# Keys laid out in DRAM by GpSimd's own stores, means of the first dense stage as three products, and low parts of keys taken later

## The chip, the cores and the metric

The kernel runs on one core of one Trainium2 chip. Its time is device time in microseconds (us) of one execution. The kernel before takes 2951.6 us, the median of three runs (2944.76 to 2952.74).

## The reference, cut to what matters

The input `x` is four images of 384 channels by 48 x 48 places (2304 tokens an image), all float32. The layer is an attention whose queries get a local part from a convolution:

```
local  = depthwise_conv_7x7(x), scaled and shifted (batch norm)
x_norm = layernorm over channels of x
q, k, v = x_norm @ qkv_w.T + qkv_b          # 8 heads of 48
q      = q + layernorm over channels of local
out    = softmax(q @ k.T / sqrt(48)) @ v    # 2304 x 2304 per head
out    = x + (out @ proj_w.T + proj_b)
```

## The kernel before

Tokens are worked on in groups of 384 (8 image rows), six groups to an image, so 24 groups `t` in all. Heads are worked on in pairs, four pairs to an image; a pair's keys against a group's queries are twelve *slots*: four pairs, three slots each, six key blocks of 128 tokens to a slot.

**Dense stage.** Ahead of the attention of an image, `from_x` (L565) is run for its six groups. TensorE makes for a group the values (3 products), the keys (3, `u` = 0 to 2) and the queries (3); in later images also the output projection of the image before (3). Products are made two at a time: `both` (L634) takes the generator through its two halves, the TensorE half and the evacuation half. The dense stage of the first image (0 to 164 us) also makes the layer norm of the next group inside each group. The norm's mean over channels was a sum of three 128-channel chunks by two VectorE additions (L404, L405) and one product with a constant matrix (`mean`, L416), once for the values and once for their squares. In later images (`kv` stages) the norm goes another way, by `out` (L460, L461: a small store to DRAM and its read back, `parts` and `four`) and `few_in` (L470), which VectorE waits for in its order.

**High and low parts of keys.** Keys are kept as a rounded part and a remainder. ScalarE writes the rounded part `k[:, 0]` (L593). VectorE writes the remainder `k[:, 1]` (L596) in `low`, which reads the PSUM tile again. `low` is put in a list; `both` runs all that are in the list between its two halves, so one `both` after its product. Then `low` calls `keys_out`, which issues the stores. The tiles `k` are taken from the same five buffers (tag `pt`) as the exponentials `pt` of the attention.

**Layout of keys.** The score products (L881) want a *stack* `ks` of a pair: 128 rows of two halves of 2304, in which each head has its 48 rounded rows, its 48 remainder rows and, for the third product, remainder rows twice. Head pairs 0, 1, 2 come mostly whole out of `u` = 0, 1, 2; heads 6 and 7 (pair 3) come in 16-row pieces of all three. `keys_out` on SyncE's queue (SP) writes pair 0 straight into its stack in SBUF (8 DMAs a group, `stack_head`, L544 to L547) and all other parts to a DRAM tensor `keys` in head order (10 DMAs a group, L531, L532). So SP issues 18 DMAs for a group's keys. In the first attention group of each image GpSimd's queue builds the stacks of pairs 1 to 3 out of `keys` by `stack_head` (8 DMAs a pair, each over all 2304 tokens), and after that stores each of the four stacks to DRAM as `wide` (`keep_stack`, L551, 2304 KB each). From then on, a stack is read from `wide` in three thirds of 768 KB (`load_keys`, L558), in every group, one pair ahead. There are two stack buffers in SBUF.

**Attention.** In a slot, TensorE makes 36 score products (L881), ScalarE exponentiates (L889) and TensorE weighs the values (L896, 24). VectorE meanwhile does the 7 x 7 convolution of the next group, 147 operations `acc` (L288) a group, spread over the slots and the dense stage by `plan` (L358), which is given an estimate of VectorE's free time per point (`spare`, `spare_at_keys`). VectorE also makes the low part of the queries (L758), after which SP copies pieces of `qs` (L763, L765). The order on TensorE, VectorE and ScalarE is the order of the text; the orders on SP and GpSimd are made by the framework's scheduler. Every engine works its own instructions in order.

Of the kernel before, what the change touches and what calls it, by code (L numbers as in the profile page):

```python
# [16 lines left out]
P = 128  # L17
NH = 8
# [27 lines left out]
def unshifted_pass(  # L46
# [333 lines left out]
    class Norm:  # L380
# [33 lines left out]
        def mean(self, m=None):  # L414
            self.m = two_banks()[:, 0, :G] if m is None else m
            nc.tensor.matmul(self.m, lhsT=mean_w, rhs=self.buf[:, 0, :], start=True, stop=True)  # L416

# [99 lines left out]
    keys, values = {}, {}  # L517
    lows = []
# [19 lines left out]
    def place_keys(b, p):  # L538
        stacks[b, p] = big.tile([P, 2, N], HALF, tag="ks", name=f"ks{b}_{p}", bufs=2)

    def stack_head(b, p, j, head, at, queue):

        dst, r = stacks[b, p].bitcast(F32), 64 * j
        queue.dma_start(out=dst[r : r + HD, 0, at], in_=head[:, 0])  # L544
        queue.dma_start(out=dst[r + HD : r + 64, 0, at], in_=head[0:16, 1])
        for i in range(2):
            queue.dma_start(out=dst[r + 32 * i : r + 32 * i + 32, 1, at], in_=head[16:HD, 1])  # L547

    def keep_stack(b, p):
        wide[b, p] = dram.tile([P, 2, N], F32, tag=f"wide{p}", name=f"wide{b}_{p}")  # L550
        nc.gpsimd.dma_start(out=wide[b, p], in_=stacks[b, p].bitcast(F32))  # L551
# [12 lines left out]

    def from_x(b, g, before=None, ao=None):  # L565
# [6 lines left out]
        if g == 0:  # L572
            keys[b] = dram.tile([NH, HD, 2, N], F32, tag="keys", name=f"keys{b}")
# [399 lines left out]
    norm.sum()  # L973
    norm.mean(bank)
# [9 lines left out]
    norm.sum_squares()  # L984
    norm.mean()
    norm.root()
    both(making)
    convolve_first(4)
    norm.scale(norm.newton())
    both(making)  # L990
    convolve_first(7)
    for g in range(1, NG):

        last = g == NG - 1
        making = from_x(0, g)
        both(making)
        assert not last or n_first >= each - PE_TAPS
        norm = Norm(accs[0] if last else xn[0, g + 1])
        norm.sum()
# [10 lines left out]
        norm.sum_squares()  # L1010
        norm.mean()
# [12 lines left out]
    query_end(0)  # L1024
    high_queries(0, 0)
    low_queries(0, 0)
    gather_tails(*reversed(queries[0]))
# [3 lines left out]
    for t in range(NT):  # L1031
        b, g = divmod(t, NG)
        if g == 0 and b:
# [4 lines left out]
            for gk in range(NG):  # L1038
# [48 lines left out]
        for s in range(NSLOT):  # L1087
# [638 lines left out]
```

## Time and profile before

| what | value |
|---|---|
| median of three runs | 2951.6 us |
| the profiled execution's own time / its span | 2951.98 / 2950.2 us |
| TensorE (PE) busy / VectorE (DVE) busy | 2783.3 us (94%) / 2474.2 us (84%) |
| ScalarE (ACT) / GpSimd (POOL) busy | 1641.8 us (56%) / 244.9 us (8%) |
| mean granted TensorE clock | 0.97 |
| DMA | 431.71 MB in 191693 packets |
| first dense stage / kv stages | 0 to 164 / about 820 to 957, 1521 to 1657, 2219 to 2360 us |

The profile is of one execution. "Busy" counts an engine's instructions; SP and POOL also issue DMAs. A row of a timeline gives start and length in us, engine, line, operation, what is written and read, and in brackets the idle time of the engine before it and what ended it. A fp32 product is two recorded matmuls, so a mean's single product is "x2" and one over three chunks is "x6". A row of a table of stretches gives a stretch's length, then each engine's busy time in it (with the number of instructions), the granted clock, the DMA engines' busy share and GB/s.

### The profile page before, as it was taken

The numbers are of one execution on the slowest core, as the hardware profiler recorded it, in microseconds if no ns is written. First come the engines' busy times: TensorE is split into PE (matmuls) and PEld (weight loads), VectorE is DVE, ScalarE is ACT, GpSimd is POOL, SyncE is SP. The second block draws the span as 40 slices with busy tenths as digits, with TensorE's granted clock in tenths as the row PEclk, the third lists the DMA queues.
The fourth block names the chain that finished last, engine by engine and source line by source line (L and its number), as shares of the span: only waits on it lengthen the run. The fifth ranks groups of instructions, "written<-read, shape, count | busy, mean of one in ns | idle before, by whom it ended". The sixth has DMA issues, their size and how long they took to land.

```text
span 2950.2 us, 52742 instructions
## 1 busy us (share of the span) xinstructions
PE 2783.3 (94%) x19190; PEld 1749.7 (59%) x19190; DVE 2474.2 (84%) x4899; ACT 1641.8 (56%) x2638; POOL 244.9 (8%) x429
## 2 busy tenths in 40 slices
PE   8868899898899899999999979999999999999999
PEld 5445555565555556666665646666665555666665
DVE  7869998898899699998999969999988978898512
ACT  4235556566532466676652446667773255666662
POOL 1011000000000100100100101001000010100100
PEclk9989999999999999999999989999999999999999
DMA  6265444443535954455445764545453675544551
GB/s 134 58 159 168 143 127 138 118 141 120 147 87 139 228 167 143 143 175 153 144 109 146 175 190 147 170 145 152 154 149 92 168 187 180 159 141 155 167 172 62
DMA packets 191693, 431.71 MB, mean 146 GB/s; under 512 B 62592, under 2 KB 139328, under 8 KB 186304
## 3 DMA queue, kind: packets, MB, share of 16 engines
q0 software_dynamic: 42016, 254.84, 26.9%
q1 hardware_dynamic: 146416, 169.80, 23.6%
q8 instruction: 154, 2.52, 0.4%
q10 hardware_dynamic: 2992, 3.62, 0.3%
q14 instruction: 115, 0.94, 0.1%
HBM read 298.44 MB, written 86.02 MB: 130 GB/s over the span
## 4 chain that ended last, share of the span: by engine, by line
PE 67%; DVE 21%; DMA 10%; SPq 1%; issue 1%; ACT 1%; ACTq 0%; DVEq 0%
PE o L896 27%; PE r L881 23%; PE r L507 16%; DVE acc L288 14%; DMA parts<-part 4%; DMA four<-parts 2%; DMA qs<-qs 1%; DMA keys<-k 1%; DMA xn<-in_x_dram 1%; DVE ao L800 1%; DMA ks<-k 1%; DVE sq L405 0%; DVE qs L758 0%; DVE sq L456 0%; DVE sq L404 0%
## 5 line engine op out<-in xcount | busy, mean ns | idle before, releaser
L288 DVE SCALAR_TENSOR_TENSOR acc<-slab,vec,acc 128x368 f32<-128x368 f32 (+6 forms) x3447 | 1770.0, 584 | 1.2
L889 ACT ACTIVATE pt<-r 128x768 f32<-128x768 f32 x1728 | 1253.9, 827 | 208.9 <-PE r L881 148.5
L896 PE MATMUL o<-pt,v 128*64 128x384 f32 x6912 | 1184.9, 492 | 1.6 <-ACT pt L889 1.5
L881 PE MATMUL r<-qs,ks 64*128 64x384 f32 x10368 | 1037.1, 349 | 137.1 <-DMA qs<-qs 67.8
L881 PEld LDWEIGHTS r<-qs,ks 64*128 64x128 f32 x10368 | 922.5, 191 | 330.0 <-issue 252.0
L896 PEld LDWEIGHTS o<-pt,v 128*64 128x64 f32 x6912 | 472.1, 137 | 596.5 <-issue 511.4
L558 POOL DMA_DIRECT2D ks<-wide x240 | 173.6, 725 | 1723.4 <-PE r L881 1658.4
L781 ACT COPY o<-o 113x384 f32<-113x384 f32 x192 | 92.2, 480 | 378.5 <-PE o L896 378.4
L507 PE MATMUL r<-xn,w_qk 128*128 128x384 f32 x864 | 283.7, 486 | 0.0
L507 PEld LDWEIGHTS r<-xn,w_qk 128*128 128x128 f32 x864 | 164.2, 190 | 114.5
L507 PE MATMUL r<-w_v,xn 128*128 128x384 f32 x432 | 153.5, 509 | 15.7 <-DVE xn L502 15.2
L470 DVE TENSOR_REDUCE few<-four 128x12 f32<-128x48 f32 x80 | 18.6, 232 | 167.8 <-DMA four<-parts 167.6
L585 ACT COPY v<-r 128x384 f32<-128x384 f32 x72 | 32.1, 481 | 216.9 <-PE r L507 216.9
L507 PEld LDWEIGHTS r<-w_v,xn 128*128 128x128 f32 x432 | 84.8, 199 | 80.0 <-DVE xn L502 18.3
L800 DVE TENSOR_TENSOR ao<-ao,o 113x384 f32<-113x384 f32 x144 | 79.7, 553 | 57.7 <-ACT o L781 57.4
L507 PE MATMUL r<-af,w_o 128*128 128x384 f32 x360 | 119.1, 487 | 0.0
L791 ACT COPY ao<-o 113x384 f32<-113x384 f32 x72 | 34.4, 478 | 122.8 <-PE o L896 122.8
L758 DVE TENSOR_TENSOR qs<-xn,qs 128x384 fp32r<-128x384 f32 x72 | 39.9, 555 | 70.4 <-ACT qs L753 70.4
L507 PEld LDWEIGHTS r<-af,w_o 128*128 128x128 f32 x360 | 68.2, 190 | 47.8 <-issue 0.6
L610 ACT ACTIVATE xn<-r,qkb 128x384 f32<-128x384 f32 x72 | 41.5, 580 | 90.7 <-PE r L507 89.0
L593 ACT ACTIVATE k<-r,qkb 128x384 fp32r<-128x384 f32 x72 | 39.4, 580 | 63.4 <-PE r L507 51.8
L862 DVE SCALAR_TENSOR_TENSOR xr<-r,pb,xr 128x384 f32<-128x384 f32 x72 | 42.1, 612 | 35.8 <-PE r L507 20.0
(124 smaller groups left out, 963.4 us busy)
## 6 DMA issues: line engine op xcount, KB each, us to landing
ks<-wide POOLq DMA_DIRECT2D x240, 768.0 KB, 7.0
wide<-ks POOLq DMA_DIRECT2D x16, 2304.0 KB, 12.1
qs<-qs SPq DMA_DIRECT2D x528, 48.0 KB
keys<-k SPq DMA_DIRECT2D x96, 144.0 KB
ks<-keys POOLq DMA_DIRECT2D x48, 288.0 KB, 12.2
xr<-in_x_dram SPq DMA_DIRECT2D x24, 576.0 KB
slab<-in_x_dram SPq DMA_DIRECT2D x32, 378.0 KB
held<-ao SPq DMA_DIRECT2D x20, 576.0 KB
```

Of the source, the lines that this page charges most:

```text
L288: nc.vector.scalar_tensor_tensor(dst, src, weight, dst, ALU.mult, ALU.add)
L507: nc.tensor.matmul(dst, lhsT=weights(c), rhs=src(c), start=c == 0, stop=c == CC - 1)
L558: nc.gpsimd.dma_start(out=stacks[b, p].bitcast(F32)[:, :, at], in_=wide[b, p][:, :, at])
L593: nc.scalar.activation(k[:, 0, :], r[:, :G], AF.Identity, bias=bias)
L610: nc.scalar.activation(src[:, i, :], q[:, :G], AF.Identity, bias=qkb[:, 0, i : i + 1])
L758: nc.vector.tensor_sub(qs[:, 1, :], query_of(t, p), qs[:, 0, :])
L781: nc.scalar.copy(part[0 : 64 + HA], sums[0 : 64 + HA, 0, :G])
L800: nc.vector.tensor_add(dst, dst, part[0 : 64 + HA])
L862: nc.vector.scalar_tensor_tensor(xr[:, co, :], m, pb[:, co : co + 1], xr[:, co, :], ALU.add, ALU.add)
L881: nc.tensor.matmul(r[:, j, :G], lhsT=ks[rows, w, kb * P : (kb + 1) * P], rhs=qs[rows, m, :], start=i == 0, stop=i == 2,)
L889: nc.scalar.activation(pt, r[:, :, :G], AF.Exp, scale=SCALE)
L896: nc.tensor.matmul(sums[halves[j], 0, :G], lhsT=values[t // NG, kb // NB][:, first : first + 64], rhs=pt[:, j, :], start=i == 0, stop=i == ...
```

## The change

1. Keys of `u` = 1, 2 and all pieces of pair 3 are stored by GpSimd's queue from SBUF straight into the stack layout in DRAM (`wide[b, 1..3]`), 32 DMAs a group. SP keeps the 8 of pair 0. The tensor `keys` is gone.
2. `load_keys` always reads `wide` by thirds, in the first group of an image too. Only pair 0's stack is still stored from SBUF (`keep_stack(b)`, once an image, after slot 1).
3. In the first dense stage both means of a norm are a product over three chunks (`mean_by_chunk`), without VectorE's additions.
4. `both` no longer runs the low parts; `lows_out(n)` stands further back: in a `kv` group the first after convolve point 2 and the other two after point 3; in the first dense stage after `root` and after ten convolution operations; of that stage's last group, two after `low_queries(0, 0)`. `spare_at_keys` is changed to match, with the same sum.

```
     def spare_at_keys(b, g, h):
-        time = 4.6 - {0: 0.6, 1: 0.7, 2: 1.4, 4: 1.2}.get(h, 0.0)
+        time = 4.6 - {0: 0.6, 2: 0.7, 3: 1.4, 4: 1.2}.get(h, 0.0)
...
+        def mean_by_chunk(self, src, m=None):
+            self.m = two_banks()[:, 0, :G] if m is None else m
+            project(self.m, lambda c: mean_w, lambda c: src[:, c, :])
...
+    def stack_head(dst, j, k, queue):
+
+        r = 64 * j
+        queue.dma_start(out=dst[r : r + HD, 0], in_=k[r : r + HD, 0])
+        queue.dma_start(out=dst[r + HD : r + 64, 0], in_=k[r : r + 16, 1])
+        for i in range(2):
+            queue.dma_start(out=dst[r + 32 * i : r + 32 * i + 32, 1], in_=k[r + 16 : r + HD, 1])
 
     def keys_out(b, g, u, k):
         at = slice(g * G, (g + 1) * G)
         k = k.bitcast(F32)
-        if u == 0:
-            if g == 0:
-                place_keys(b, 0)
-            for j in range(2):
-                stack_head(b, 0, j, k[64 * j : 64 * j + HD], at, nc.sync)
+        if g == u == 0:
+            place_keys(b, 0)
+            for p in range(1, NP):
+                wide[b, p] = dram.tile([P, 2, N], F32, tag=f"wide{p}", name=f"wide{b}_{p}")
         for j in range(2):
-            r = 64 * j
-            if u:
-                nc.sync.dma_start(out=keys[b][2 * u + j, :, :, at], in_=k[r : r + HD])
-            nc.sync.dma_start(
-                out=keys[b][6 + j, 16 * u : 16 * u + 16, :, at], in_=k[r + HD : r + 64]
-            )
...
+            if u == 0:
+                stack_head(stacks[b, 0].bitcast(F32)[:, :, at], j, k, nc.sync)
+            else:
+                stack_head(wide[b, u][:, :, at], j, k, nc.gpsimd)
+        for j in range(2):
+            last, r = wide[b, NP - 1][64 * j : 64 * j + 64, :, at], 64 * j + HD
+            nc.gpsimd.dma_start(out=last[16 * u : 16 * u + 16, 0], in_=k[r : r + 16, 0])
+            if u == 0:
+                nc.gpsimd.dma_start(out=last[HD:64, 0], in_=k[r : r + 16, 1])
+                continue
+            for i in range(2):
+                to = 32 * i + 16 * (u - 1)
+                nc.gpsimd.dma_start(out=last[to : to + 16, 1], in_=k[r : r + 16, 1])
...
     def load_keys(b, p, i):
+        at = slice(i * BATCH * P, (i + 1) * BATCH * P)
         if i == 0:
             place_keys(b, p)
-        if (b, p) in wide:
-            at = slice(i * BATCH * P, (i + 1) * BATCH * P)
-            nc.gpsimd.dma_start(
-                out=stacks[b, p].bitcast(F32)[:, :, at], in_=wide[b, p][:, :, at]
-            )
-        elif i == 0:
-            for j in range(2):
-                stack_head(b, p, j, keys[b][2 * p + j], slice(0, N), nc.gpsimd)
+        nc.gpsimd.dma_start(out=stacks[b, p].bitcast(F32)[:, :, at], in_=wide[b, p][:, :, at])
...
     def both(making):
-        due = list(lows)
-        lows.clear()
         next(making)
-        for low in due:
-            low()
         next(making)
+
+    def lows_out(n):
+        for _ in range(n):
+            lows.popleft()()
...
         norm = Norm(accs[0] if last else xn[0, g + 1])
-        norm.sum()
-        norm.mean()
+        norm.mean_by_chunk(norm.src)
...
-        norm.sum_squares()
-        norm.mean()
+        norm.mean_by_chunk(norm.buf)
         norm.root()
+        lows_out(1)
         if last:
             both(making)
         both(making)
         convolve_first(6 if last else 10)
+        if not last:
+            lows_out(2)
...
     low_queries(0, 0)
+    lows_out(2)
     gather_tails(*reversed(queries[0]))
...
                 convolve("kv", t, gk, 2)
+                lows_out(1)
...
                 convolve("kv", t, gk, 3)
+                lows_out(2)
...
-            if g == 0 and third == 1:
-                keep_stack(b, pair)
             if pair < NP - 1 or g < NG - 1:
                 load_keys(b, (pair + 1) % NP, third)
+            if s == 1 and g == 0:
+                keep_stack(b)
```

More of the change, by code (lines that the diff above doesn't have):

```diff
@@ L515, in gather_tails, with place_keys @@
                 )
-    keys, values = {}, {}
-    lows = []
+    values = {}
+    lows = deque()
+    stacks, wide = {}, {}
+    def place_keys(b, p):
+        stacks[b, p] = big.tile([P, 2, N], HALF, tag="ks", name=f"ks{b}_{p}", bufs=2)
+        return stacks[b, p].bitcast(F32)
+    def stack_head(dst, j, k, queue):
[4 more added lines that the diff above has]
+            queue.dma_start(out=dst[r + 32 * i : r + 32 * i + 32, 1], in_=k[r + 16 : r + HD, 1])
     def keys_out(b, g, u, k):
@@ L536, in unshifted_pass @@
-    stacks, wide = {}, {}
[L538 to L547, printed above, removed]
@@ L549, in keep_stack @@
-    def keep_stack(b, p):
-        wide[b, p] = dram.tile([P, 2, N], F32, tag=f"wide{p}", name=f"wide{b}_{p}")
-        nc.gpsimd.dma_start(out=wide[b, p], in_=stacks[b, p].bitcast(F32))
+        if g == u == 0:
+            place_keys(b, 0)
+            for p in range(1, NP):
+                wide[b, p] = dram.tile([P, 2, N], F32, tag=f"wide{p}", name=f"wide{b}_{p}")
+        for j in range(2):
+            if u == 0:
+                stack_head(stacks[b, 0].bitcast(F32)[:, :, at], j, k, nc.sync)
+            else:
+                stack_head(wide[b, u][:, :, at], j, k, nc.gpsimd)
@@ new lines, in keys_out, with keep_stack @@
+        for j in range(2):
[7 more added lines that the diff above has]
+                nc.gpsimd.dma_start(out=last[to : to + 16, 1], in_=k[r : r + 16, 1])
+    def keep_stack(b):
+        wide[b, 0] = dram.tile([P, 2, N], F32, tag="wide0", name=f"wide{b}_0")
+        nc.gpsimd.dma_start(out=wide[b, 0], in_=stacks[b, 0].bitcast(F32))
@@ L571, in from_x @@
         values[b, g] = flat
-        if g == 0:
-            keys[b] = dram.tile([NH, HD, 2, N], F32, tag="keys", name=f"keys{b}")
         nc.gpsimd.memset(v[:, :, :, HD:HA], 1.0)
@@ L972, in unshifted_pass @@
     norm = Norm(xn[0, 1])
-    norm.sum()
-    norm.mean(bank)
+    norm.mean_by_chunk(norm.src, bank)
     convolve_first(12)
@@ L988, in unshifted_pass @@
     convolve_first(4)
+    lows_out(3)
     norm.scale(norm.newton())
@@ L998, in unshifted_pass @@
         norm = Norm(accs[0] if last else xn[0, g + 1])
-        norm.sum()
-        norm.mean()
+        norm.mean_by_chunk(norm.src)
         if last:
@@ L1009, in unshifted_pass @@
             both(making)
-        norm.sum_squares()
-        norm.mean()
+        norm.mean_by_chunk(norm.buf)
         norm.root()
+        lows_out(1)
         if last:
```

## The prediction

> **What bounds the kernel now.** I read the page's busy shares and chain first, then a table of stretches, then timelines of the places where TensorE stands.
>
> ```profile
> PE 2783.3 (94%) x19190; PEld 1749.7 (59%) x19190; DVE 2474.2 (84%) x4899; ACT 1641.8 (56%) x2638; POOL 244.9 (8%) x429
> PE 67%; DVE 21%; DMA 10%; SPq 1%; issue 1%; ACT 1%; ACTq 0%; DVEq 0%
> ```
>
> TensorE is the bound: it is idle for 2950.2 - 2783.3 = 167 us, and a change can win little more than those. The table says where they lie (length, PE busy, then DVE after PEld; at the end clock, DMA share, GB/s).
>
> ```profile
> 0.00:165.00 165.00, 145.28 (x500) 88.08 (x500) 125.81 (x254) 62.15 (x136) 12.76 (x43) 0.95 0.47 98
> 165.00:188.30 23.30, 0.69 (x3) 0.33 (x3) 18.04 (x34) 0.51 (x1) 3.67 (x8) 0.54 0.96 214
> 188.30:470.00 281.70, 249.32 (x1881) 160.23 (x1881) 254.52 (x495) 160.45 (x242) 26.90 (x43) 0.92 0.52 148
> ...
> 957.00:1074.00 117.00, 98.70 (x735) 61.72 (x733) 91.75 (x180) 62.42 (x95) 18.61 (x34) 0.94 0.82 214
> 1074.00:1521.00 447.00, 444.42 (x3599) 285.02 (x3599) 413.48 (x831) 308.56 (x486) 39.81 (x64) 0.99 0.49 148
> ...
> 1657.00:1750.00 93.00, 76.55 (x557) 48.11 (x555) 66.16 (x131) 47.59 (x73) 15.77 (x30) 0.91 0.87 212
> ...
> 2360.00:2465.00 105.00, 92.41 (x708) 58.73 (x708) 82.89 (x162) 60.91 (x94) 15.91 (x29) 0.95 0.81 213
> ```
>
> Idle: 20 us in the dense stage, 22.6 before the first scores, about 63 in the rest of image 0 (where VectorE is over 90% busy), and 18.3 + 16.5 + 12.6 = 47.4 in the first attention groups of images 1 to 3. The five groups after such a group lose 2.6 together (1074 to 1521). What sets the first groups apart is the DMA share: 0.81 to 0.87 against 0.49. The chain names the transfers.
>
> ```profile
> 163.06 13.25 DMA keys<-k
> 176.33 11.88 DMA qs<-qs
> 188.26 5.98 PE r L881 x35
> ...
> 999.87 26.43 DMA parts<-part
> ```
>
> Before the first scores, SP's stores of keys and then the copies of `qs` behind them. In image 1 a 6 KB `parts` store takes 26.43 us, VectorE waits for it in its order, ScalarE behind VectorE and TensorE behind ScalarE:
>
> ```profile
> 1012.72 4.57 PE L881 MATMUL r<-qs,ks 64*128 64x384 f32 x31 [3.46 <-DMA qs<-qs]
> 1017.23 4.09 PE L896 MATMUL o<-pt,v 128*64 128x384 f32 x24
> 1021.25 1.84 PE L881 MATMUL r<-qs,ks 64*128 64x384 f32 x18
> 1032.52 3.41 PE L881 MATMUL r<-qs,ks 64*128 64x384 f32 x18 [9.44 <-ACT ao L791]
> ```
>
> **Part 1, first groups of images 1 to 3.** Removed there: three of four `keep_stack` writes (3 x 2304 KB) and three stack builds of 2304 KB in long rows. Added: the same stacks by thirds as in any group, and part of pair 1's already fetched during the kv stage. In 957 to 1074 that takes 7 MB of writes out of 214 GB/s x 117 us = 25 MB, and the builds no longer come in bursts. What stays is one 2304 KB write near the start. I take these groups to behave like 1074 to 1521: half a us a group, 1.5 to 2 of the 47.4 stays. Gain 45; bounds 0 (the waits have another cause) and 57, since after each stall TensorE also ran slower (31 matmuls in 4.57 or 5.46 us, not about 2.9), some 4 us an image.
>
> **Part 2, the added wait.** A tile `k` is a buffer of `pt`, and the exponentials of a first slot reuse those of the last group's keys. The fourth needs the stores of `u` = 1 landed and the fifth those of `u` = 2. In image 1 the two lows stood at 953.6 to 954.7 with nine convolutions behind them (to 959.3); now they come after these, at about 959. Behind them are 10 + 10 stores on GpSimd. No row shows such a store from GpSimd; the nearest is its stack build:
>
> ```profile
> L547 POOL DMA_DIRECT2D ks<-keys x48: 492/500/514, 165.7 to 2406.5; - x48
> ```
>
> 20 x 0.5 = 10 us, plus about 3 to land (small loads by GpSimd landed in 3.4 to 4.2 us at the start), makes 972. TensorE begins scores at 961.3, takes 4.0, weighs four blocks (2.7), and is at 968 when it wants the fifth `pt`: 972 + 0.8 - 968 = 4.8 us of stall. Behind this exponential on ScalarE are the sixth and the copies of sums. Three images: +14; bounds 0 and 3 x 15.
>
> Per group GpSimd now issues 32 stores, 16 us at 0.5, and half a load of 0.7, in a group of 22.8 us (137/6). So it keeps up if a store costs no more than 0.7. In the built program each GpSimd DMA waits for the one eight before it, so the price is the larger of 0.5 and an eighth of the landing. Two rules speak against the change. The Trainium skill, "DMA: Bandwidth & Descriptors", in "Rules for kernel authors", calls transfers under 64 KB mostly overhead, with about 2.0 us fixed (its "Anatomy of one DMA"): 32 in sequence would be 64 us a group, 41 too many, over 900 us in 24 groups. With eight in flight the same 2.0 us are 0.25 each, under the 0.5 of the row: I take the row. Its section "SWDGE vs HWDGE vs iDMA" says that GpSimd writes its descriptors to SBUF and is locked out while VectorE runs in a two-port mode. The row speaks to that: between 209.2 and 213.2 eight builds took 0.50 or 0.51 each while VectorE's `acc` ran without a gap. By the rule the price would lie above 0.5, by an amount no row gives; I keep 0.5.
>
> **Part 3, start of the attention.** VectorE's low part of the queries was done at 168.5, and the first full run of scores began at 188.26, 19.8 us later. Stores of keys stood ahead of the copies in SP's queue (the last took 2.20 us to issue, since the landing of earlier ones was late) while GpSimd's write of 2304 KB and two bursts of builds filled the engines (share 0.96). Now SP holds pair 0's 8, long issued, and a few `qt` copies: about 1.5 us more of issue, 3.6 for six copies, 2 to land, so 7 us after. The fifth exponential needs 20 GpSimd stores that begin right after the low queries, partly behind the 2304 KB write: 15 to 17 us after, when TensorE wants it at some 15. So 12.8 gained, about 1 given back: 12 us. Bounds: 4 (`qs` again late) to 15. VectorE, idle 16.16 us at 183 to 199 for this start, moves with it; after 199 it is nearly gapless, so in the rest of image 0 I count nothing.
>
> **Part 4, means in the dense stage.** Removed: 6 norms x 2 means x 2 additions x 0.555 = 13 us of VectorE. Added: 12 x (2.10 - 0.81) = 15.5 us of TensorE.
>
> ```profile
> 90.91 5.83 PE L507 MATMUL r<-w_v,xn 128*128 128x384 f32 x12 [2.73 <-DVE xn L502]
> 96.57 0.81 PE L416 MATMUL r<-sq,mean_w 128*128 128x384 f32 x2
> 97.22 2.10 PE L507 MATMUL r<-w_v,xn 128*128 128x384 f32 x6
> ```
>
> Groups started at 45.5, 67.5, 90.9, 115.7, 140.2; TensorE waited about 3 to 4 us in each for the next `xn`, and then ran twelve matmuls in 5.83 us that take 4.03 without a wait before them. Without gaps its work is about 18.9 + 2.6 = 21.5 us. VectorE's is about 19 to 21 less 2.2, and it also loses its waits for ScalarE in front of `low` (22.8 us in the whole run, mostly here), since `low` comes later. So TensorE sets 21.5: gains 0.5 + 1.9 + 3.3 + 3.0 = 8.7; the first norm costs about 1.5, the last group gets 1.5 back by the clock. Sum -9; bounds -12 and +15 (nothing hidden).
>
> **Part 5, at nothing.** Ten SP issues fewer a kv group (6 us): TensorE is idle 1 us in a kv stage. Low parts later hold two PSUM buffers longer; in that stage's groups the later of them would end 3 us or more before its buffer's next product. If VectorE falls back by that much, TensorE waits for the difference; up to 3 us a kv stage. The new split of the planner has the same sum.
>
> **Sum.** -9 - 12 - 45 + 14 = -52 on the execution's own 2951.98 us: 2900 us. The median of the runs shown is 2951.6, so nothing is shifted.
>
> **Rivals.** *Half of it*: the first groups' waits are only halved, since VectorE is late there for itself (91.75 of 117 us busy) and the fetched thirds still delay `parts`: -24 in place of -45, 2923. The means not being hidden (+15 for -9) would give the same 2924. For it: the end of that group also waits on `qs` behind convolutions; against it: the 26.43 us row. *Nothing left*: all those waits stay, 2945. *Slower, GpSimd's queue becomes the bound*: if a store costs r, a group's queue takes 32r and the delay beyond 22.8 us piles up until ScalarE waits for a `k` or `pt` buffer. From r = 0.71 it grows by 32(r - 0.71) a group, 24 groups; it has eaten the 66 us gained at r = 0.80, a landing of 6.4 us. At r = 0.85 it costs 107: about 3007. For it: thirds of 768 KB land in 7 us in the same queue, and stack builds landed in 10 to 12. Against it: those were in the crowded stretches, while the dense stages have a share of 0.2 to 0.5.
>
> **How the numbers follow.** The change does as said: 0.58, 2880 to 2915 by the bounds that are likely together. Half: 0.18. Nothing: 0.06. Slower: 0.18. Differences under 0.3% can't be told from none for this kernel. So faster 0.76, same 0.06, slower 0.18. The range runs from 2872 (clock regained, stalls of part 2 absent) to 2946, leaving the slower case out.
>
> **What would show it.** Right: GpSimd's stores at 0.5 us back to back, `parts` no longer 12 to 26 us in the first groups, their DMA share near 0.6, TensorE idle under 5 us each but for one wait of about 5 in the first slot, on `wide<-k`; first scores some 20 us earlier; dense groups of 21.5 us with "x6" means. Wrong: GpSimd issues spread over 0.8 us or more, ScalarE's `k` or `pt` waiting for `wide<-k` by tens of us, or `parts` as late as before.

## The result, and the profile after

The changed kernel takes 2857.6 us, the median of four runs (2855.57 to 2861.88), beside 2951.8 for the kernel before (2944.76 to 2952.74, four runs): a ratio of 0.9688, with a 95% interval of 0.9668 to 0.9707. It gains 94 us where 52 were forecast, and 2857.6 lies below the range of 2872 to 2946. The profiled execution took 2855.57 us, its span is 2853.8.

The page of the changed kernel, its busy shares and its chain:

```profile
PE 2769.0 (97%) x19238; PEld 1740.4 (61%) x19238; DVE 2459.7 (86%) x4875; ACT 1636.8 (57%) x2638; POOL 592.9 (21%) x1125
PE 78%; DVE 14%; DMA 5%; issue 1%; ACT 0%; SPq 0%; POOL 0%; ACTq 0%; DVEq 0%; POOLq 0%
```

TensorE's idle time fell from 167 us to 85, and its own busy time fell by 14 us, although it does more products than before. The share of transfers in the chain went from 10% to 5%. GpSimd, with 1125 instructions and not 429, is busy 593 us and has no weight in the chain.

The table of stretches of the changed kernel (length; busy us and number of instructions of PE, PEld, DVE, ACT, POOL; granted clock, DMA share, GB/s): the dense stage, the start of the attention, the same length of image 0 as was shown of before, then the first group of image 1, the five groups behind it, and the first groups of images 2 and 3.

```profile
0.00:156.50 156.50, 151.85 (x548) 94.06 (x548) 115.45 (x231) 61.92 (x135) 98.18 (x216) 1.00 0.56 120
156.50:166.30 9.80, 0.68 (x2) 0.28 (x1) 8.73 (x18) 0.98 (x2) 5.43 (x12) 0.68 0.88 309
166.30:448.00 281.70, 248.13 (x1889) 158.61 (x1891) 264.32 (x515) 162.21 (x247) 26.72 (x40) 0.93 0.44 127
931.91:1020.53 88.62, 88.62 (x721) 56.65 (x720) 85.75 (x168) 60.36 (x93) 15.97 (x27) 1.00 0.54 167
1020.53:1468.36 447.83, 444.54 (x3602) 282.61 (x3600) 413.89 (x832) 308.15 (x487) 39.70 (x64) 1.00 0.50 150
1607.88:1696.37 88.49, 88.49 (x722) 56.69 (x722) 84.43 (x166) 60.44 (x93) 15.57 (x26) 1.00 0.53 167
2283.16:2371.61 88.45, 88.45 (x721) 57.04 (x720) 82.22 (x160) 60.43 (x93) 14.92 (x25) 1.00 0.53 160
```

The first groups are now gap-free: PE busy equals the length, the clock is 1.00, and the DMA share is 0.53 or 0.54 where it was 0.81 to 0.87. The dense stage ends at 156.5, not 164.1, and from there to the first full run of scores it is 9.8 us, not 24.1. Image 0's stretch is as empty as it was (33.6 us of idle against 32.4).

The small transfer that held these groups up is quick now. The `parts` store of image 1's first group landed after 26.43 us; the one in the changed kernel has landed when SP issues the read of `four` behind it, 2.5 us later. What VectorE waited for these two in that group (total us, times), of before and then of the changed kernel:

```profile
  DVE few L470: 24.6, 1
...
  DVE few L474: 0.3, 1
```

Adding up the whole span by stage gives the 96.4 us between the two spans. A group's length is counted from its first score product to the next group's or stage's; 88.27 is the length of an undisturbed one.

| stage | before | after | gain |
|---|---|---|---|
| from the start to the first full run of scores | 188.3 | 166.3 | 21.9 |
| from there to the end of image 0 | 632.0 | 626.0 | 6.0 |
| three kv stages | 420.1 | 418.6 | 1.5 |
| first and second groups of images 1 to 3, above 6 x 88.27 | 79.2 | 0.7 | 78.5 |
| the eleven groups behind them, above 11 x 88.27 | 1.6 | 12.4 | -10.8 |
| last group | 128.5 | 129.1 | -0.6 |

Where a stall of the first scores was, the chain of the changed kernel (start, length, what) now has this:

```profile
162.99 3.36 DMA qs<-qs
166.35 5.19 PE r L884 x35
```

The copies of `qs` take 3.36 us to land, not 11.88. TensorE's timeline in the dense stage and in the first slots of image 1 (start, length, engine, line, operation, number, and idle time before it in brackets where there is any):

```profile
90.49 4.03 PE L511 MATMUL r<-w_v,xn 128*128 128x384 f32 x12
94.36 2.10 PE L511 MATMUL r<-xn,mean_w 128*128 128x384 f32 x6
...
931.91 3.62 PE L884 MATMUL r<-qs,ks 64*128 64x384 f32 x36
935.46 4.09 PE L899 MATMUL o<-pt,v 128*64 128x384 f32 x24
939.48 3.41 PE L884 MATMUL r<-qs,ks 64*128 64x384 f32 x36
```

The twelve products of values no longer wait and take 4.03, the means are "x6", and groups start at 47.9, 69.2, 90.5, 111.8, 133.1, every 21.3 us. In image 1 the scores, the weighing and the next scores follow without a gap: the wait of part 2 isn't there. The stores on GpSimd's queue, in the list of tile `wide` (shortest, median and longest ns of an issue):

```profile
L536 POOL DMA_DIRECT2D wide<-k x192: 496/506/791, 44.2 to 2285.2; - x192
L558 POOL DMA_DIRECT2D wide<-k x192: 484/487/789, 47.0 to 2287.6; - x192
```

They cost the 0.5 us taken from the row of before. The 480 stores of 24 KB land in 2.1 us (median).

### The profile page after: what moved, and what is told of

The parts are those of the page before. It is cut to its first block, busy times and chain, and to the rows that moved or that the text cites. A ratio compares the mean times of both kernels' runs of the same rounds, so it can differ in the third digit from the quotient of the medians.

```text
span 2853.8 us, 53591 instructions
## 1 busy us (share of the span) xinstructions
PE 2769.0 (97%) x19238; PEld 1740.4 (61%) x19238; DVE 2459.7 (86%) x4875; ACT 1636.8 (57%) x2638; POOL 592.9 (21%) x1125
## 4 chain that ended last, share of the span: by engine, by line
PE 78%; DVE 14%; DMA 5%; issue 1%; ACT 0%; SPq 0%; POOL 0%; ACTq 0%; DVEq 0%; POOLq 0%
PE o L899 32%; PE r L884 26%; PE r L511 20%; DVE acc L288 10%; DMA parts<-part 2%; DMA four<-parts 2%; DMA qs<-qs 1%; DVE sq L405 0%; DVE sq L460 0%; DVE ao L803 0%; DVE part L461 0%; DMA start_up<-in_qkv_wT_dram 0%; DVE sq L404 0%; DVE acc L482 0%; DVE ao L1155 0%
## 5 line engine op out<-in xcount | busy, mean ns | idle before, releaser
L884 PE MATMUL r<-qs,ks 64*128 64x384 f32 x10368 | 1016.7, 345 | 67.0 <-DMA qs<-qs 38.9
L884 PEld LDWEIGHTS r<-qs,ks 64*128 64x128 f32 x10368 | 905.9, 188 | 256.9 <-issue 210.6
L568 POOL DMA_DIRECT2D ks<-wide x276 | 199.3, 724 | 1819.4 <-PE r L884 1768.6
L511 PEld LDWEIGHTS r<-xn,w_qk 128*128 128x128 f32 x864 | 164.3, 190 | 114.3
L511 PE MATMUL r<-w_v,xn 128*128 128x384 f32 x432 | 145.1, 488 | 0.7 <-ACT w_v L697 0.5
L803 DVE TENSOR_TENSOR ao<-ao,o 113x384 f32<-113x384 f32 x144 | 79.4, 551 | 54.8 <-ACT o L784 54.7
L536 POOL DMA_DIRECT2D wide<-k x192 | 96.7, 508 | 9.2 <-issue 5.5
L558 POOL DMA_DIRECT2D wide<-k x192 | 93.1, 491 | 9.5 <-DMA wide<-k 6.8
L552 POOL DMA_DIRECT2D wide<-k x144 | 70.6, 493 | 97.6 <-ACT k L596 69.2
```

What stands on the lines that cost most here:

```text
L511: nc.tensor.matmul(dst, lhsT=weights(c), rhs=src(c), start=c == 0, stop=c == CC - 1)
L536: queue.dma_start(out=dst[r + 32 * i : r + 32 * i + 32, 1], in_=k[r + 16 : r + HD, 1])
L552: nc.gpsimd.dma_start(out=last[16 * u : 16 * u + 16, 0], in_=k[r : r + 16, 0])
L558: nc.gpsimd.dma_start(out=last[to : to + 16, 1], in_=k[r : r + 16, 1])
L568: nc.gpsimd.dma_start(out=stacks[b, p].bitcast(F32)[:, :, at], in_=wide[b, p][:, :, at])
L803: nc.vector.tensor_add(dst, dst, part[0 : 64 + HA])
```

## The experiments

Each kernel is timed beside the kernel before on the same chip, so the ratios compare: the changed kernel's is 0.9688 (0.9668 to 0.9707). The medians of the kernel before were 2953.7 us with the first four experiments, 2948.1 with the next four and 2956.6 with the last four.

### The old traffic brought back

The theory: the first groups were slow because of the volume of traffic that the old layout moved there (stack writes and long stack builds), which delays small transfers. The rivals: SP's shorter queue, or the moved low parts, is what helped. All three kernels keep the change and add traffic; the additional writes go to a tensor that nobody reads.

`both_again`:

```
+    def keep_again(b, p):
+        spill = dram.tile([P, 2, N], F32, tag=f"spill{p}", name=f"spill{b}_{p}")
+        nc.gpsimd.dma_start(out=spill, in_=stacks[b, p].bitcast(F32))
...
+        if first:
+            if i == 0:
+                ks = stacks[b, p].bitcast(F32)
+                for r in (0, 64):
+                    for lo, hi, half in ((0, HD, 0), (HD, 64, 0), (0, 32, 1), (32, 64, 1)):
+                        nc.gpsimd.dma_start(
+                            out=ks[r + lo : r + hi, half], in_=wide[b, p][r + lo : r + hi, half]
+                        )
+            return
...
+            if g == 0 and third == 1 and pair:
+                keep_again(b, pair)
-                load_keys(b, (pair + 1) % NP, third)
+                load_keys(b, (pair + 1) % NP, third, g == 0 and pair < NP - 1)
```

> The changed kernel with the old traffic of an image's first attention group put back, and SP's queue left short: stacks of pairs 1 to 3 are fetched whole by eight DMAs each, and each is written once more to DRAM (2304 KB, to a tensor that nobody reads). Theory 1, big transfers delay the small ones that VectorE and TensorE wait for: first groups of images 1 to 3 go back from 88.5 to 105 to 116 us, their successors to 90 to 94, and the run gains 60 to 80 us, 2920 to 2940. Theory 2, what helped is SP's queue having 10 DMAs fewer a group: first groups stay under 95 us and the time under 2880.

`writes_again` has `keep_again` and its call alone:

> Only the three extra writes of 2304 KB in each image's first group are put back. Theory 1 in the form that the writes do it: about two thirds of the first groups' 78 us come back, 2900 to 2925. In the form that the builds' bursts do it: under 15 us, 2860 to 2872. Theory 2 (SP's queue): no change, 2855 to 2862.

`builds_again` has the other half, the stacks of pairs 1 to 3 built by eight long-row DMAs at once in first groups:

> Only the fetch of whole stacks by eight DMAs in each image's first group is put back, in place of thirds. Theory 1 in the form that the writes do it: under 15 us, 2858 to 2872. In the form that bursts do it: 40 us or more, above 2895. Theory 2: no change.

| kernel | median (lowest to highest), us | ratio (95%) | first and second groups, above 88.27 | eleven groups behind |
|---|---|---|---|---|
| changed | 2857.6 (2855.57 to 2861.88) | 0.9688 (0.9668 to 0.9707) | 0.7 | 12.4 |
| `writes_again` | 2886.3 (2870.74 to 2896.51) | 0.9752 (0.9717 to 0.9787) | 25.4 | 29.5 |
| `builds_again` | 2892.1 (2883.36 to 2905.39) | 0.9779 (0.9745 to 0.9814) | 35.0 | 23.4 |
| `both_again` | 2932.8 (2925.62 to 2936.54) | 0.9931 (0.9908 to 0.9954) | 64.9 | 17.1 |
| before | 2953.7 (2947.62 to 2961.86) | 1 | 79.2 | 1.6 |

The last two columns are of one profiled execution each: the slowest of the four of `writes_again` (2896.51 us) and of `builds_again` (2905.39), the fastest of `both_again` (2925.62). The table of stretches of `both_again`, its first groups of images 1 to 3:

```profile
933.13:1041.71 108.58, 93.94 (x721) 60.99 (x720) 81.26 (x159) 61.51 (x93) 24.13 (x46) 0.92 0.80 213
1639.41:1754.50 115.09, 95.13 (x722) 61.86 (x721) 80.61 (x158) 61.55 (x93) 24.15 (x46) 0.88 0.72 200
2341.88:2441.74 99.86, 93.02 (x722) 60.30 (x722) 77.35 (x151) 61.40 (x93) 23.29 (x45) 0.95 0.86 229
```

One row of its TensorE timeline in the first of them, a piece of its chain, and two rows of SP's timeline:

```profile
1017.46 5.58 PE L897 MATMUL r<-qs,ks 64*128 64x384 f32 x32 [11.45 <-DMA qs<-qs]
...
996.60 18.07 DMA parts<-part
...
1014.68 0.58 SPq L465 DMA_DIRECT2D four<-parts  x1
1015.37 1.15 SPq L781 DMA_DIRECT2D qs<-qs  x2
```

With the traffic back and nothing else, the groups are nearly as long as before, at about the clock, DMA share and GB/s of before. TensorE stands 11.45 us for copies of `qs`, but it isn't these copies that are slow: VectorE had made their data by 1000.1, and they were issued at 1015.37, since the read of `four` stood ahead of them in SP's queue until the `parts` store had landed, after 18.07 us. So one small store that the traffic delays holds up what stands behind it in its queue.

This gives back 64 of the 78.5 us in these groups, 75 us in all by the medians (72 by the ratios). The writes alone give back 25 and the builds alone 34 of the 64 in their profiled executions, which are the slowest of each; by the ratios of all executions they give back 19 and 27 of the 72. So neither is the cause alone, and whether the two simply add isn't shown. What the remaining 14 us are, 8 of them in the first group of image 3, stays open. That the traffic is the main cause is shown. SP's shorter queue and the later low parts, which this kernel keeps, leave it nearly as slow as before; at most those 14 us are left to them in these groups.

### The stores on SP's queue

```
-                stack_head(wide[b, u][:, :, at], j, k, nc.gpsimd)
+                stack_head(wide[b, u][:, :, at], j, k, nc.sync)
...
-            nc.gpsimd.dma_start(out=last[16 * u : 16 * u + 16, 0], in_=k[r : r + 16, 0])
+            nc.sync.dma_start(out=last[16 * u : 16 * u + 16, 0], in_=k[r : r + 16, 0])
```

(and the two stores behind it likewise).

> The stores of keys into the stacks' layout are issued by SP in place of GpSimd, all else as changed. SP then has 40 DMAs a group at 0.6 us, 24 us, more than a group of 21.3 to 23.3 us: the queue should fall behind in each dense stage, delay parts, four and the copies of queries, and cost 20 to 60 us, 2880 to 2920, with first scores at 175 us or later. If which queue issues makes no difference, the time stays within 5 us of 2858.

It takes 2973.6 us (2971.34 to 2986.64), ratio 1.0077 (1.0051 to 1.0103): 116 us more than the changed kernel and 0.8% slower than the kernel before, so this expectation was far too mild. Its first scores missed the other way: the first full run begins at 167.3, not at 175 or later. The first kv stage in its table of stretches:

```profile
794.53:967.72 173.19, 149.26 (x435) 84.87 (x434) 130.81 (x254) 34.23 (x72) 1.69 (x5) 0.94 0.42 113
```

and what VectorE waits for in it, in its list of waits (total us, times, longest):

```profile
DVE few L474 <- DMA four<-parts: 40.2, 5, 9.8
```

A kv stage of 139.5 us takes 173.2, 160.6 and 160.2 (75.4 us more in the three), and the first groups behind them lose 42. An issue of such a store costs SP less than GpSimd (0.42 us in the median in this stage), and SP issues for 134 us of the 173 (65 of 139.5 in the changed kernel), so the queue isn't full. But it works in order: the store and the read back of `parts` now stand behind stores of keys (VectorE had finished the last `part` of this stage at 915.0, and its store was issued at 922.9, behind fourteen stores of keys), and VectorE waits for the read, 8 us each time. On this queue the new layout is a loss; what it gains, it gains on a queue where nothing urgent stands behind the stores.

### Twice the stores on GpSimd's queue

```
                 stack_head(wide[b, u][:, :, at], j, k, nc.gpsimd)
+                stack_head(spare_of[b, u][:, :, at], j, k, nc.gpsimd)
-        for j in range(2):
-            last, r = wide[b, NP - 1][64 * j : 64 * j + 64, :, at], 64 * j + HD
+        for j, of in ((0, wide), (1, wide), (0, spare_of), (1, spare_of)):
+            last, r = of[b, NP - 1][64 * j : 64 * j + 64, :, at], 64 * j + HD
```

> Every store of keys that GpSimd issues is issued twice (the second to a tensor that nobody reads): 64 a group. My rival's mechanism: 32 us of issue in a group of 21.3 to 23.3 us, so the queue falls behind by about 10 us a group, until ScalarE waits for a buffer of k after about 1.5 groups: 25 to 45 us an image, 2960 to 3040. If the wait for buffers has more room than that, or the stores overlap better: under 2900.

It takes 3105.6 us (3102.18 to 3115.36), ratio 1.053 (1.0486 to 1.0575). The first kv stage and the group behind it in its table of stretches:

```profile
835.97:996.19 160.22, 141.88 (x435) 82.94 (x433) 128.29 (x248) 34.09 (x72) 132.56 (x273) 0.95 0.51 137
996.19:1130.72 134.53, 97.11 (x720) 61.05 (x720) 86.35 (x168) 62.00 (x94) 66.60 (x130) 0.84 0.52 150
```

TensorE's timeline in that group:

```profile
1022.47 1.33 PE L886 MATMUL r<-qs,ks 64*128 64x384 f32 x6 [11.94 <-ACT pt L894]
```

and ScalarE's waits over both:

```profile
ACT k L598 <- DMA spare<-k: 35.0, 6, 16.4
ACT pt L894 <- DMA wide<-k: 15.2, 2, 11.7
```

This is the slower rival, wait for wait: GpSimd is busy 132.6 of 160 us, ScalarE waits for a `k` or `pt` buffer whose stores haven't landed, and TensorE behind it. Doubling the stores is the rival's r = 1.0 us; its formula, 32 x (1.0 - 0.71) us in each of 24 groups, gives 223, and the kernel takes 248 us more than the changed one (by the spans 44 up to the end of image 0, 59 in the kv stages, 144 in the groups behind them). The 2960 to 3040 expected was too low. So the mechanism is real and its formula comes near at this one price; where it turns, 0.71, wasn't measured. At the real 0.5 us the queue has room.

### Parts of the dense stage, one at a time

`means_back` undoes the three-product means:

```
-    norm.mean_by_chunk(norm.src, bank)
+    norm.sum()
+    norm.mean(bank)
...
-    norm.mean_by_chunk(norm.buf)
+    norm.sum_squares()
+    norm.mean()
```

(and likewise in the groups behind).

> The changed kernel with the means of the first dense stage made as before, by VectorE's two additions and one product. If the products gain because TensorE's gaps go: groups of that stage last 22 to 23.5 us in place of 21.3, the stage ends 5 to 9 us later, 2863 to 2867. If the earlier low parts alone made the gain, TensorE saves its 2.6 us a group and the stage ends up to 8 us earlier, 2850.

`lows_early` undoes the later low parts (and the planner's split, which belongs to them):

```
     def both(making):
+        due = list(lows)
+        lows.clear()
         next(making)
+        for low in due:
+            low()
         next(making)
     def lows_out(n):
-        for _ in range(n):
-            lows.popleft()()
+        pass
```

> The changed kernel with the low parts of keys made one half earlier again, between the halves of the next pair of products, and the planner's table to match. If VectorE's waits for ScalarE in front of them were part of the dense stage's loss: 3 to 8 us more there, 2861 to 2866. If the later place only delays the stores: the first slot's exponentials wait less, and the time is 0 to 6 us less.

`dense_back` undoes both:

> The changed kernel with both halves of part 4 undone: the means of the dense stage as additions on VectorE and one product, and the low parts of keys where they were (with the planner's old split). Nothing is left out. It is the fourth corner of a square whose other three are known by the start of the first full run of scores: 166.3 us with both edits (the changed kernel), 158.2 with the later low parts alone, 175.6 with the three-product means alone. If the two edits add up, this corner stands at 175.6 + 158.2 - 166.3 = 167.4 and the three-product means cost 8 us wherever the low parts are. If the means are paid for only where TensorE bounds the stage (my present theory: with later low parts it is TensorE's, with early ones VectorE's), then VectorE's additions count here: the groups run at 22 to 25 us as before, the scores start at 172 to 176, and the means are worth 0 to 3 us in this corner. Time: some 5 us above or below the kernel with the early low parts by the second theory, 8 below it by the first.

`means_alone` is the kernel before with the three-product means as its only edit (the opposite of `means_back`'s diff, made in the kernel before):

> The kernel before with one edit: the means of the dense stage as three products each. Nothing is left out. By part 4 of the prediction this alone should end the dense stage up to 9 us earlier (155), for a time some 9 us under the kernel before. By what the runs have shown since, the low parts and not the means set the stage's pace: then its groups stay at 22 to 25 us, the dense stage ends at 162 to 168 and the time is the kernel before's within 5 us.

| kernel | low parts | means | first full run of scores, us | median (lowest to highest), us | ratio (95%) |
|---|---|---|---|---|---|
| changed | later | three products | 166.3 | 2857.6 (2855.57 to 2861.88) | 0.9688 (0.9668 to 0.9707) |
| `means_back` | later | additions | 158.2 | 2847.7 (2840.43 to 2853.93) | 0.9646 (0.9604 to 0.9688) |
| `lows_early` | early | three products | 175.6 | 2868.1 (2862.49 to 2874.15) | 0.9717 (0.9675 to 0.9758) |
| `dense_back` | early | additions | 172.7 | 2869.8 (2865.96 to 2872.5) | 0.97 (0.9672 to 0.9728) |
| before | early | additions | 188.3 | 2951.8 (2944.76 to 2952.74) | 1 |
| `means_alone` | early | three products | 191.5 | 2977.5 (2972.73 to 2978.47) | 1.0064 (1.0042 to 1.0087) |

TensorE's timeline at the products of values, of `means_back`:

```profile
83.42 4.03 PE L511 MATMUL r<-w_v,xn 128*128 128x384 f32 x12
...
102.96 4.14 PE L511 MATMUL r<-w_v,xn 128*128 128x384 f32 x12 [0.67 <-DVE xn L506]
```

of `lows_early`:

```profile
92.91 4.14 PE L511 MATMUL r<-w_v,xn 128*128 128x384 f32 x12 [1.44 <-DVE xn L506]
...
117.32 5.83 PE L511 MATMUL r<-w_v,xn 128*128 128x384 f32 x12 [2.86 <-DVE xn L506]
```

and of `dense_back`:

```profile
91.17 5.83 PE L511 MATMUL r<-w_v,xn 128*128 128x384 f32 x12 [2.74 <-DVE xn L506]
...
115.98 5.61 PE L511 MATMUL r<-w_v,xn 128*128 128x384 f32 x12 [4.15 <-DVE xn L506]
```

The first full run of scores is read from one profiled execution each. The later low parts do the work. With them VectorE's `xn` is in time or nearly so (with the additions TensorE waits 0.67 and 1.51 us in the last two groups of `means_back`); without them TensorE waits 1.4 to 4.2 us for it in a group. What they take away is in VectorE's lists of waits between 45 and 140 us (total us, times, longest), of before:

```profile
DVE k L596 <- ACT k L593: 13.9, 8, 2.3
```

of the changed kernel:

```profile
DVE k L599 <- ACT k L596: 5.0, 3, 1.9
```

of `means_back`:

```profile
DVE k L599 <- ACT k L596: 0.2, 1, 0.2
```

and of `dense_back`, where the low parts are early again (`lows_early` has 19.7 us of this wait):

```profile
DVE k L599 <- ACT k L596: 13.5, 7, 2.3
```

A low part that follows its product closely has VectorE wait for ScalarE's rounded part, and `xn` behind it is late. Once this is gone TensorE bounds the stage: groups of 21.3 us in the changed kernel and 18.8, 19.3 and 19.5 in `means_back`, a difference near the 2 x (2.10 - 0.81) = 2.6 us that the means add to TensorE. (The last group of `means_back` takes 21.7: there TensorE waits for VectorE again.) So the low parts gain 14.5 us at the first scores with additions and 9.2 with products; the three-product means cost 8.1 and 2.9. By the first scores they are a loss with either place of the low parts; over the whole time the intervals of each pair overlap (the changed kernel and `means_back`, `lows_early` and `dense_back`). `dense_back`, as its second theory had it, shows that the two edits don't simply add. `means_alone` agrees: groups of about 23 to 26 us, the first full run of scores 3.2 us later, and 21 us more in all. By its spans only 4.5 of these come before the end of image 0; the others are scattered over the stalls of later stages (8 in the first and second groups, 6 behind them, 3 in the first kv stage), which this edit doesn't touch and for which I have no reason. The expectation of "within 5 us" missed.

The comparison of `dense_back` with before gives the start of the attention by itself: the dense stage ends where it did (164.3 and 164.1 us), and the first full run of scores comes 15.5 us earlier. Which part of the change does this, SP's shorter queue or the traffic of GpSimd's, no run separates. The means and low parts make the other 6.4 of the 21.9.

### The planner's split

```
-        time = 4.6 - {0: 0.6, 2: 0.7, 3: 1.4, 4: 1.2}.get(h, 0.0)
+        time = 4.6 - {0: 0.6, 1: 0.7, 2: 1.4, 4: 1.2}.get(h, 0.0)
```

> Only the planner's table of free time in the kv stages as before. Groups 10 and 16 took 93.3 and 93.7 us in the changed kernel and 88.3 before. If they come from where the table puts the convolutions: both at 88.3, the time 10 us less, 2847. If not: the same within 3 us.

2854.3 us (2847.6 to 2855.92), ratio 0.967 (0.9633 to 0.9707): no difference that can be told. The two groups asked about still take 92.6 and 92.3 us, so the table isn't what made them long.

### The wait of part 2, pushed

```
                 convolve("kv", t, gk, 3)
-                lows_out(2)
...
                 convolve("kv", t, gk, 4)
+                lows_out(2)
```

> The changed kernel with two of the three low parts of keys in a kv group one place further back, behind the fourth stretch of convolutions. Nothing is left out. In image 1 this puts the last group's two low parts one addition and seven convolutions later, 0.6 + 7 x 0.52 = 4.2 us, and so all 20 stores behind them. It measures the wait of part 2. In the changed kernel the stores of the second tile landed 1.0 us before the fourth exponential of the next stage began, and those of the third tile about 2 us before the eighth did. If that wait is as these figures say, the first slots of images 1 to 3 now show ScalarE waiting 2 to 4 us for a store and the first groups become 90 to 92 us in place of 88.5: 5 to 11 us in all. If the wait has more room than that, or if TensorE is covered by the blocks of scores it has in hand, the groups stay at 88.5 and the time at the changed kernel's. If it is as the prediction had it (fifth exponential), each group loses 4 us more than that: over 15 in all.

2864.3 us (2859.86 to 2866.83), ratio 0.9686 (0.9659 to 0.9714), the changed kernel's. First groups of images 1 to 3: 89.0, 89.0 and 93.2 us, not 88.6, 88.5 and 88.5. Only image 3's loses something. Its ScalarE timeline:

```profile
2294.40 1.51 ACT L892 ACTIVATE pt<-r 128x768 f32<-128x768 f32 x2 [0.77 <-DMA wide<-k]
2299.01 0.81 ACT L892 ACTIVATE pt<-r 128x768 f32<-128x768 f32 x1 [3.10 <-DMA wide<-k]
```

and its GpSimd timeline:

```profile
2289.96 0.49 POOL L558 DMA_DIRECT2D wide<-k  x1 [2.64 <-DMA wide<-ks]
```

The expectation took the fourth and eighth exponentials for fixed. They aren't: the tiles are dealt from five buffers in the order in which the program allocates them, and with the low parts elsewhere the second and third tile's buffers come to the tenth exponential and to the twelfth to fourteenth. In image 1 the edit delayed the stores of both tiles by about 8 us (4.2 were expected), and the exponentials that wait for them by as much. So it doesn't measure the margin of the changed kernel's wait, which stays at what its trace shows: in image 1 the last store of the second tile had landed at 934.3 when the fourth exponential began at 934.9. The 4.8 us that image 3 lost have another origin as well: the 2304 KB write now went out ahead of these stores, the first seven of them landed in 5.7 to 7.2 us, not 2.1, and GpSimd, which has eight DMAs under way, stood 2.64 and 0.86 us. The wait exists, and it takes such a neighbour to bring it up.

### Small reads beside a burst

The 10.8 us lost in the eleven other groups are two groups of the changed kernel, the fifth of images 1 and 2, which take 93.3 and 93.7 us, not 88.3. VectorE's timeline in the first, after:

```profile
1336.05 0.23 DVE L474 TENSOR_REDUCE few<-four 128x12 f32<-128x48 f32 x1 [8.01 <-DMA four<-parts]
```

and in the same group of before:

```profile
1389.05 0.24 DVE L470 TENSOR_REDUCE few<-four 128x12 f32<-128x48 f32 x1 [3.25 <-DMA four<-parts]
```

`means_back_x1` is `means_back` with the input loads of the next image, which stand next to this read on SP's queue, a slot later:

```
-            if s == 0 and coming:
+            if s == 1 and coming:
```

> The changed kernel with the means of the dense stage as additions on VectorE again (which by itself gave a ratio of 0.9646) and the loads of the next image's input one slot later. Nothing is left out. In two groups of the changed kernel (the fifth of images 1 and 2) VectorE waited 8 us for the small load of four, because its store went out with a burst of three stack loads and three loads of input; each such group took 93.3 to 93.7 us, not 88.3. If the loads of input are what delays it, both groups go back to 88.3 and the time falls by 5 to 10 us below the 2847.7 of the kernel with the means alone undone, to about 2840. If the three stack loads are enough, the groups stay at 93 and the time at about 2848.

2858.5 us (2852.03 to 2861.94), ratio 0.9663 (0.9639 to 0.9688), `means_back`'s within the intervals, and the groups stay at 93.3 and 93.5. But the edit doesn't do what it is for. SP's timeline in the first of them:

```profile
1323.65 0.58 SPq L465 DMA_DIRECT2D four<-parts  x1
1324.28 0.94 SPq L94 DMA_DIRECT2D xn<-in_x_dram  x2
```

The loads still go out 0.6 us behind the read, in both groups, as in `means_back`. So this run says nothing of them. The kernel before does: its loads follow the read by as little (0.64 and 0.63 us), VectorE waits 3.3 us in both groups, and both take 88.3. Input loads next to the read aren't enough to make a group long.

What separates the groups is in the traces of the kernels (thirteen kernels, `stores_twice` left out, two groups each; in 23 of the 26 a read of `four` was issued within 5 us of the first of GpSimd's three stack loads of 768 KB). In the six where it was issued at most 0.61 us after that load's issue, VectorE waited 2.8 to 4.6 us; in the seventeen where it was 0.70 us or more, 6.9 to 8.6 us, and the group was 92 to 96 us long. Five of the six were 88.3; in the sixth, the first of `means_back_x1`, TensorE waited 3.06 us for copies of `qs` instead. The kernel before fell on the early side twice (0.38 us after, and 0.03 before), the changed one on the late side twice (1.25 and 1.61). So this loss looks like a matter of phase (of when the read happens to meet the loads) and not of an edit. That rests on the sorting alone; no run moved one read on purpose.

## Why the prediction was wrong

**What bounds the kernel** was read rightly: TensorE's idle time and the stalls of its own after them were what could be won, and the first groups of images 1 to 3 held most of it.

**Part 1, first groups: right in mechanism, a term too small.** Forecast 45 with bounds of 0 and 57, measured 78.5. The step that failed is the size of what could be won there, 47.4: the working undercounted what stood in its own rows, twice. The stretches that gave 47.4 us of idle were cut at 1750 and 2465, where the first group of image 2 ran to 1777 and the second groups of images 1 and 3 had stalls too (94.2 and 90.4 us): whole groups hold 54.7. And the step "since after each stall TensorE also ran slower ... some 4 us an image" went into the bound alone, as 12 us. By the busy time of TensorE in those groups, over the 88.27 that the same work takes undisturbed, it is 5.7 + 2.9 + 8.3 + 5.5 + 2.1 = 24.5, and all of it came back with the stalls. 54.7 + 24.5 = 79.2, of which 0.7 stays. `both_again` shows that the traffic is what costs most of it. The 33.5 us by which this part was short are most of the 44 by which the sum was, counted by the spans. The 14 us of part 2, which never came, are the next largest; smaller gains and losses nearly cancel.

**Part 2, the added wait: wrong.** Forecast 14, measured under 1. The step that failed is "the fourth needs the stores of `u` = 1 landed and the fifth those of `u` = 2". In the built program the fourth and the eighth have those buffers, and the order of allocation decides that; the eighth comes after the stores have landed. The times given to the stores erred to the late side: in image 1 the low parts ended 3.5 us before the scores began (2 were assumed), the 20 stores were issued in 9.7 us (10), and the last landed 7.3 us into the first slot (10.7). The price of a store, 0.5 us, was right, and so was taking it over the 2.0 us that the Trainium skill ("DMA: Bandwidth & Descriptors", "Anatomy of one DMA") gives as fixed: the 2.1 us measured here is the time to landing, with eight under way. The lock-out of GpSimd beside VectorE isn't seen in this kernel's medians of 487 and 506 ns; whether VectorE was in the mode that it needs, no run shows.

**Part 3, start of the attention: near**, 12 forecast. `dense_back` gives 15.5, just over the upper bound of 15: with the wait of part 2 absent, nothing is given back. That the copies land sooner is seen (3.36 us, not 11.88); which of the causes named in this part made it isn't separated.

**Part 4, the dense stage: the sum near, the reason wrong.** Forecast -9, measured -6.4 at the first scores (15.5 to 21.9); the stage itself ends 7.6 earlier. The period of 21.5 us was right (21.3), and so was "TensorE sets" it. The step that failed is to credit this to the removed additions, and not to ask what the stage would do without the edit: with the low parts later, TensorE would have had 18.9 us of work by the same line, and VectorE, additions and all, keeps up with that in three groups of four (18.8, 19.3, 19.5 and 21.7). The clause on VectorE's "waits for ScalarE in front of `low`" held the gain. The three-product means are a loss of 3 to 8 us at the first scores.

**Part 5, at nothing: near.** The kv stages gained 1.5. The 6.0 us in the rest of image 0 and the 10.8 lost later weren't foreseen. The first stays unexplained: from the first score product on, image 0 took 623 to 637 us in these kernels (`stores_twice` apart) without a cause that I traced.

**The rivals.** *Half of it* and *Nothing left* fall with the first groups. *Slower* is a real mechanism, its cost near the formula's at twice the stores, that the changed kernel doesn't reach.

The version with the means undone has the earliest first scores, 8.1 us ahead of the changed kernel's, and the lowest ratio, 0.9646 (0.9604 to 0.9688). Over the whole time it can't be told from the changed kernel, whose interval overlaps it.

## What to carry to other kernels

Cost a stage that stalls by its whole length against the same work undisturbed, not by the idle time in it: here a third of what came back was TensorE running slower after the stalls. Where two edits meet in one stage, work out each without the other before crediting it, since the one may move the bound that the other is paid at. And a wait on a pool's buffer is found in the built program: which instruction inherits the buffer changes with the order of allocation.

## What the hardware showed that was not expected

TensorE's slow run after a wait doesn't follow from the length of the wait alone. Twelve products of 384 columns that take 4.03 us without a wait take 4.14 after waits of 0.56 to 2.13 us in these traces, with a granted clock of 1.00, and 5.6 to 7.1 after waits of 2.82 us and more, with a granted clock of 0.58 to 0.73. In between, both happen: `dense_back` has 5.83 us after 2.74 us of idle (shown above, granted clock 0.71), and `lows_early` this (granted clock 1.00):

```profile
143.31 4.14 PE L511 MATMUL r<-w_v,xn 128*128 128x384 f32 x12 [2.74 <-DVE xn L506]
```

Two runs of eighteen products were slowed already after 2.25 and 2.29 us (7.77 us, not 5.97, in `means_alone` and `sp_stores`).

A 24 KB read that was issued 0.7 us or more after the first of three 768 KB loads of another queue had VectorE waiting 6.9 to 8.6 us; one issued at most 0.61 us after it, 2.8 to 4.6 us.
